# Every dense float32 product of a two-layer graph network written as two products of 64 columns of the tensor array

## The chip, the cores and the metric

The kernel runs on one core of a Trainium2 chip. The metric is the time on the device in microseconds (us), the median of repeated runs.

Names used below: PE is the tensor engine, PEld its weight loads, DVE the vector engine, ACT the scalar engine, POOL the GpSimd engine. A "slot" is the 429 ns that lie, in these traces, between the starts of two records of PE with 512 columns of a float32 operand; a float32 product leaves two records, one slot each.

## The reference

Two layers over a batch of 32 graphs of 512 nodes with 512 features, all float32. Layer 0 is masked attention with 8 heads of 64, layer 1 a graph attention whose logits are a sum of two vectors.

```python
# layer 0
h = relu(layernorm(x));  q, k, v = h @ Wq + bq, h @ Wk + bk, h @ Wv + bv      # 8 heads of 64
attn = softmax(q @ k.T / 8 + (1 - adj) * -1e9)
x = x + (attn @ v) @ Wo + bo
# layer 1
h = relu(layernorm(x));  g = h @ W;  s1, s2 = g @ a1, g @ a2
att = softmax(leaky_relu(s1[:, None] + s2[None, :], 0.2) * adj)
x = x + elu(att @ g + beta * g)
```

## The kernel before

PE's order is written by hand; the other engines follow a scheduler. While batch b is in its attention, PE also works on the projections of batch b+1 (pq, pk, pv), on the output projection of b-1 (pw) and on the second layer of b-2 (pg, py). These are the dense products: weights of 128 columns, four steps of accumulation. The functions that matter (lines left out are marked `# ...`):

```python
def proj_q(b, hT, f, qT):                       # proj_k, proj_v, out_proj, gather, final alike
    p = psum.tile([P, N], F32, name=f"pq_{b}_{f}", tag="mm")      # tag mm: two buffers
    for c in range(C):
        nc.tensor.matmul(p, wq[:, c, ts(f, P)], hT[c], start=c == 0, stop=c == C - 1)
    q = wtile([P, N], f"qT_{b}_{f}", "qT", 6)
    nc.vector.scalar_tensor_tensor(q, p, bq_c[:, f : f + 1], edge8, op0=ALU.add, op1=ALU.mult)
    # ...

def scores(b, j, k, st):                        # two heads: 64 rows of the array each
    # ...
    for s in range(2):
        rows = slice(s * HD, (s + 1) * HD)
        nc.tensor.matmul(p[:, s, :], st["kT"][j][rows, ts(k, P)], st["qT"][j][rows, :], start=True, stop=True)
    # ... mask on DVE, exp on ACT, sum on POOL

def attend(b, j, st):                           # two heads: 64 columns of the array each
    # ...
    for k in range(T):
        for s in range(2):
            nc.tensor.matmul(po[s * HD : (s + 1) * HD, :], v[k][:, (2 * j + s) * HD : (2 * j + s + 1) * HD],
                             e[k][:, s, :], start=k == 0, stop=k == T - 1)
    # ...
    for s in range(2):
        nc.tensor.matmul(pd[s * HD : (s + 1) * HD, :], ones[:, :HD], st["es"][j][:, s, :], start=True, stop=True)
    # ...

def residual(b, st):
    # ...
    for t in range(T):
        r = wtile([P, D], f"x1_{b}_{t}", "x1", 6)
        nc.sync.dma_start(r, x[b, ts(t, P), :])
        nc.gpsimd.tensor_tensor(r, r, c_row, op=ALU.add)          # c_row = bo + bv @ Wo
        st["x1"].append(r)

# out_proj, behind its product: DVE adds p to x1, statistics on DVE, power -0.5 on POOL, nb on DVE,
# hn on ACT, two reductions on DVE. logits: the reductions are spread by pbs (lg below), a product with ones.

        # dense(b): Y final, F projections pq/pk in turn, V pv, W out_proj, G gather, lg logits, D diagonal (pe), L loads
            order = (
                G + [Y[0], F[0], Y[1], F[1], W[0], Y[2], W[1], F[2], W[2], Y[3], W[3], F[3], F[4]]
                + L + [F[5]] + lg + [F[6], F[7]] + V[:2] + D + V[2:]
            )
```

## Time and profile before

| | before |
|---|---|
| time, median | 4092.1 us (4090.8 to 4092.1, 3 runs) |
| span of the profiled run | 4089.3 us, clock 0.993 |
| PE busy | 3950.5 us, 11616 records |
| changes of tiling in PE's records (without the one-column product of a check at the end) | 768 |
| PE's wait of pbs for DVE (qT) | 35.2 us, 28 times |

The lines stand in the prediction. Three things about reading them. An instruction's tiling is the pair in front of its shapes: `128*64` is 128 rows by 64 columns of the array. A busy time overlaps: records are longer (0.59 us) than their spacing, so PE's pace is read from starts. And a time "before" an instruction in brackets is idle time of the engine, with who ended it.

### The profile page before, as it was taken

Reading aid. Unit: us, or ns where it says so; the run is one execution under the profiler, and the core shown is the slowest. Engines: PE = TensorE matmul, PEld = TensorE weight load, DVE = VectorE, ACT = ScalarE, POOL = GpSimd, SP = SyncE. Lnnn points to the kernel's source line nnn. Section 1 sums busy time; section 2 is a strip of 40 time slices with the busy share of each in tenths; the row PEclk is TensorE's granted clock in tenths of the full one; section 3 lists DMA queues with packets and bytes.
Section 4 is the critical chain, followed back from the end, with each engine's and each line's share of the span. In section 5 each row is a group of like instructions: output and inputs, shape, how many; then the busy total and the mean of one; then the engine's idle time right before and its main releaser. Section 6 shows DMA issues by size and latency. Waiting matters only on the chain. (4 is left out here: it accounts for less than half of the span.)

```text
span 4089.3 us, 32221 instructions
## 1 busy us (share of the span) xinstructions
PE 3950.5 (97%) x11616; PEld 1590.1 (39%) x11616; DVE 2409.2 (59%) x3323; ACT 1254.4 (31%) x1799; POOL 1839.0 (45%) x1519
## 2 busy tenths in 40 slices
PE   6999999999999999999999999999999999999988
PEld 3333334333343333343333433333433334333333
DVE  4556655566655566555666555665556665556653
ACT  1333323333223333233332233332333322333331
POOL 2444544444444445444444444454444444444451
PEclk9999999999999999999999999999999999999989
DMA  3000000000000000000010000000000000000000
GB/s 116 11 16 26 21 31 28 25 21 31 21 31 26 26 21 21 31 27 26 21 31 21 31 26 22 26 21 31 28 25 21 31 21 31 26 26 11 21 21 27
DMA packets 59047, 109.90 MB, mean 27 GB/s; under 512 B 6464, under 2 KB 6464, under 8 KB 58880
## 3 DMA queue, kind: packets, MB, share of 16 engines
q1 hardware_dynamic: 55872, 101.74, 7.9%
q10 hardware_dynamic: 2640, 5.24, 0.4%
q8 instruction: 93, 1.52, 0.2%
q0 software_dynamic: 368, 0.79, 0.1%
q14 instruction: 74, 0.61, 0.0%
HBM read 74.19 MB, written 33.55 MB: 26 GB/s over the span
## 5 line engine op out<-in xcount | busy, mean ns | idle before, releaser
L264 POOL TENSOR_TENSOR es<-es,e 128x512 f32<-128x512 f32 x512 | 713.2, 1423 | 460.7 <-ACT e L257 460.7
L254 DVE TENSOR_TENSOR e<-ps,nmT 128x1024 f32<-128x1024 f32 x512 | 606.3, 1216 | 457.5 <-PE ps L250 453.2
L257 ACT ACTIVATE e<-e 128x1024 f32<-128x1024 f32 x512 | 540.5, 1056 | 920.3 <-DVE e L254 743.1
L285 DVE RECIPROCAL rd<-pd 128x512 f32<-128x512 f32 x128 | 429.4, 3355 | 443.3 <-PE pd L279 443.3
L250 PE MATMUL ps<-qT,kT 64*128 64x512 f32 x2048 | 519.9, 622 | 4.0 <-DVE e L254 3.2
L222 PE MATMUL pq<-hT,wq 128*128 128x512 f32 x1024 | 467.8, 600 | 14.6 <-ACT kT L234 13.9
L377 PE MATMUL py<-w,gT 128*128 128x512 f32 x1024 | 475.6, 608 | 0.3 <-DVE qT L224 0.3
L264 POOL TENSOR_TENSOR es<-e,e 128x512 f32<-128x512 f32 x256 | 343.8, 1363 | 282.5 <-ACT e L257 282.5
L272 PE MATMUL po<-e,v 128*64 128x512 f32 x2048 | 468.8, 600 | 0.0
L232 PE MATMUL pk<-hT,wk 128*128 128x512 f32 x1024 | 467.2, 599 | 0.8 <-DVE at L334 0.8
L303 PE MATMUL pw<-wo,oT 128*128 128x512 f32 x1024 | 462.5, 595 | 3.2 <-DVE x L307 3.2
L367 PE MATMUL pg<-at,hn 128*128 128x512 f32 x1024 | 458.5, 601 | 0.0
L240 PE MATMUL pv<-wv,hT 128*128 128x512 f32 x1024 | 455.3, 597 | 0.0
L288 POOL TENSOR_TENSOR oT<-oT,rd 128x512 f32<-128x512 f32 x128 | 171.3, 1338 | 625.2 <-DVE rd L285 544.8
L297 POOL TENSOR_TENSOR x<-x,c_row 128x512 f32<-128x512 f32 x128 | 165.0, 1290 | 378.1 <-DMA x<-in_x_dram 333.5
L323 DVE CUSTOM_DVE_ANT_0 scr<-hn,wa_r 128x512 f32<-128x512 f32 x256 | 267.8, 1083 | 68.9 <-ACT hn L317 68.9
L222 PEld LDWEIGHTS pq<-hT,wq 128*128 128x128 f32 x1024 | 189.9, 190 | 280.6 <-issue 213.4
L250 PEld LDWEIGHTS ps<-qT,kT 64*128 64x128 f32 x2048 | 174.9, 187 | 313.0 <-issue 218.3
L377 PEld LDWEIGHTS py<-w,gT 128*128 128x128 f32 x1024 | 186.3, 191 | 283.1 <-issue 235.4
L367 PEld LDWEIGHTS pg<-at,hn 128*128 128x128 f32 x1024 | 190.3, 191 | 264.7 <-issue 232.4
L232 PEld LDWEIGHTS pk<-hT,wk 128*128 128x128 f32 x1024 | 189.3, 190 | 265.7 <-issue 218.0
L303 PEld LDWEIGHTS pw<-wo,oT 128*128 128x128 f32 x1024 | 194.7, 191 | 251.4 <-issue 244.7
(95 smaller groups left out, 3213.7 us busy)
## 6 DMA issues: line engine op xcount, KB each, us to landing
x<-in_x_dram SPq DMA_DIRECT2D x256, 256.0 KB, 2.9
out_dram<-y SPq DMA_DIRECT2D x128, 256.0 KB, 2.9
wq<-in_L_gnn_Wq_dram ACTq DMA_DIRECT2D x1, 1024.0 KB, 7.5
wk<-in_L_gnn_Wk_dram ACTq DMA_DIRECT2D x1, 1024.0 KB, 14.4
adj<-in_adj_dram SPq DMA_DIRECT2D x4, 256.0 KB, 11.9
wv<-in_L_gnn_Wv_dram ACTq DMA_DIRECT2D x1, 1024.0 KB, 11.8
wo<-in_L_gnn_Wo_dram ACTq DMA_DIRECT2D x1, 1024.0 KB, 14.5
w<-in_L_gnn_W_dram ACTq DMA_DIRECT2D x1, 1024.0 KB, 12.9
```

Source lines behind the costliest of these rows:

```text
L222: nc.tensor.matmul(p, wq[:, c, ts(f, P)], hT[c], start=c == 0, stop=c == C - 1)
L232: nc.tensor.matmul(p, wk[:, c, ts(f, P)], hT[c], start=c == 0, stop=c == C - 1)
L240: nc.tensor.matmul(p, hT[c][:, ts(t, P)], wv[:, c, :], start=c == 0, stop=c == C - 1)
L250: nc.tensor.matmul(p[:, s, :], st["kT"][j][rows, ts(k, P)], st["qT"][j][rows, :], start=True, stop=True)
L254: nc.vector.tensor_tensor(e, p, nmT[:, k, :].unsqueeze(1).to_broadcast([P, 2, N]), op=ALU.add)
L257: nc.scalar.activation(e, e, AF.Exp)
L264: nc.gpsimd.tensor_tensor(es[:, s, :], one[:, s, :], e[:, s, :], op=ALU.add)
L272: nc.tensor.matmul(po[s * HD : (s + 1) * HD, :], v[k][:, (2 * j + s) * HD : (2 * j + s + 1) * HD], e[k][:, s, :], start=k == 0, stop=k == ...
L285: nc.vector.reciprocal(rd, pd)
L303: nc.tensor.matmul(p, st["oT"][c][:, ts(t, P)], wo[:, c, :], start=c == 0, stop=c == C - 1)
L367: nc.tensor.matmul(p, st["hn"][k][:, ts(c, P)], st["at"][k], start=k == 0, stop=k == T - 1)
L377: nc.tensor.matmul(p, st["gT"][c][:, ts(t, P)], w1[:, c, :], start=c == 0, stop=c == C - 1)
```

## The change

The intent is to have the dense products in the tiling of the value products (128*64), with both column halves of the array at work at once. The arithmetic is the same.

```diff
+def product(nc, out, lhsT, rhs, start=True, stop=True):
+    for s in range(0, out.shape[0], HD):
+        nc.tensor.matmul(out[s : s + HD], lhsT[:, s : s + HD], rhs, start=start, stop=stop)

     def proj_q(b, hT, f, qT):
         p = psum.tile([P, N], F32, name=f"pq_{b}_{f}", tag="mm")
         for c in range(C):
-            nc.tensor.matmul(p, wq[:, c, ts(f, P)], hT[c], start=c == 0, stop=c == C - 1)
+            product(nc, p, wq[:, c, ts(f, P)], hT[c], start=c == 0, stop=c == C - 1)
 ...  # the same in proj_k, proj_v, out_proj, gather, final, diagonal (pe), row_bcast (pbs) and row_constants
```

The transposes (pn), which stay 128*128, and the scores (ps), which stay 64*128, are untouched.

More of the change, by code (lines that the diff above doesn't have):

```diff
@@ L113, in row_bcast @@
         p = psum.tile([P, N], F32, name="pb" + name, tag="mm")
-        nc.tensor.matmul(p, ones, dg.rearrange("p t n -> p (t n)"), start=True, stop=True)
+        product(nc, p, ones, dg.rearrange("p t n -> p (t n)"), start=True, stop=True)
         return p
@@ L169, in row_constants @@
             nc.vector.tensor_copy(r, bv_c[:, c : c + 1].to_broadcast([P, P]))
-            nc.tensor.matmul(p, r, wo[:, c, :], start=c == 0, stop=c == C - 1)
+            product(nc, p, r, wo[:, c, :], start=c == 0, stop=c == C - 1)
         nc.vector.tensor_add(c_row, c_row, p)
@@ L231, in proj_k @@
         for c in range(C):
-            nc.tensor.matmul(p, wk[:, c, ts(f, P)], hT[c], start=c == 0, stop=c == C - 1)
+            product(nc, p, wk[:, c, ts(f, P)], hT[c], start=c == 0, stop=c == C - 1)
         k = wtile([P, N], f"kT_{b}_{f}", "kT", 6)
@@ L239, in proj_v @@
         for c in range(C):
-            nc.tensor.matmul(p, hT[c][:, ts(t, P)], wv[:, c, :], start=c == 0, stop=c == C - 1)
+            product(nc, p, hT[c][:, ts(t, P)], wv[:, c, :], start=c == 0, stop=c == C - 1)
         s = wtile([P, D], f"v_{b}_{t}", "v", 8)
@@ L302, in out_proj @@
         for c in range(C):
-            nc.tensor.matmul(
-                p, st["oT"][c][:, ts(t, P)], wo[:, c, :], start=c == 0, stop=c == C - 1
+            product(
+                nc, p, st["oT"][c][:, ts(t, P)], wo[:, c, :], start=c == 0, stop=c == C - 1
             )
@@ L349, in diagonal @@
         for t in range(T):
-            nc.tensor.matmul(pd[:, t, :], st["as"][:, ts(t, P)], ones[:, :HD], start=True, stop=True)
+            product(nc, pd[:, t, :], st["as"][:, ts(t, P)], ones[:, :HD], start=True, stop=True)
         bd = wtile([P, T], f"bd_{b}", "bd", 2)
@@ L366, in gather @@
         for k in range(T):
-            nc.tensor.matmul(
-                p, st["hn"][k][:, ts(c, P)], st["at"][k], start=k == 0, stop=k == T - 1
+            product(
+                nc, p, st["hn"][k][:, ts(c, P)], st["at"][k], start=k == 0, stop=k == T - 1
             )
@@ L376, in final @@
         for c in range(C):
-            nc.tensor.matmul(
-                p, st["gT"][c][:, ts(t, P)], w1[:, c, :], start=c == 0, stop=c == C - 1
+            product(
+                nc, p, st["gT"][c][:, ts(t, P)], w1[:, c, :], start=c == 0, stop=c == C - 1
             )
```

## The prediction

> **What bounds the kernel now.** I read the page first, its busy shares and the slices, then the costliest groups. Tensor engine (PE) is busy in nearly every slice; no other engine passes 59%.
>
> ```profile
> PE 3950.5 (97%) x11616; PEld 1590.1 (39%) x11616; DVE 2409.2 (59%) x3323; ACT 1254.4 (31%) x1799; POOL 1839.0 (45%) x1519
> PE   6999999999999999999999999999999999999988
> L222 PE MATMUL pq<-hT,wq 128*128 128x512 f32 x1024 | 467.8, 600 | 14.6 <-ACT kT L234 13.9
> L250 PE MATMUL ps<-qT,kT 64*128 64x512 f32 x2048 | 519.9, 622 | 4.0 <-DVE e L254 3.2
> L272 PE MATMUL po<-e,v 128*64 128x512 f32 x2048 | 468.8, 600 | 0.0
> ```
>
> Three tilings of the array are in use: 128*128 (six dense groups like pq, 1024 records each; a float32 product leaves two), 64*128 (scores ps) and 128*64 (value products po and the denominators pd). Note that 2048 of the half-width records cost what 1024 full ones do: 468.8 against 467.8 us. So they must run two at a time. The busy share hides the question that matters, which is the spacing of starts, so I went to the timeline of PE in one batch, and to that of the weight loads.
>
> ```profile
> 1961.78 3.65 PE L272 MATMUL po<-e,v 128*64 128x512 f32 x16
> 1965.26 1.03 PE L279 MATMUL pd<-es,ones 128*64 128x512 f32 x4
> 1966.22 3.70 PE L232 MATMUL pk<-hT,wk 128*128 128x512 f32 x8
> 1969.76 3.60 PE L222 MATMUL pq<-hT,wq 128*128 128x512 f32 x8
> 1973.28 1.99 PE L250 MATMUL ps<-qT,kT 64*128 64x512 f32 x8
> 1975.20 3.70 PE L232 MATMUL pk<-hT,wk 128*128 128x512 f32 x8
> 1980.09 1.13 PE L114 MATMUL pbs<-dgs,ones 128*128 128x512 f32 x2 [1.18 <-DVE qT L224]
> ...
> 2004.50 1.11 PE L350 MATMUL pe<-ones,as 128*128 128x64 f32 x8
> 2005.45 7.08 PE L240 MATMUL pv<-wv,hT 128*128 128x512 f32 x16
> 2012.37 0.60 PE L214 MATMUL pn<-ident,x 128*128 128x128 f32 x4
> 2013.22 1.15 PE L214 MATMUL pn<-ident,x 128*128 128x128 f32 x8 [0.25 <-ACT v L242]
> ```
>
> ```profile
> 2006.36 0.19 PEld L240 LDWEIGHTS pv<-wv,hT 128*128 128x128 f32 x1 [0.24 <-issue]
> 2006.79 0.19 PEld L240 LDWEIGHTS pv<-wv,hT 128*128 128x128 f32 x1 [0.24 <-issue]
> 2007.22 0.19 PEld L240 LDWEIGHTS pv<-wv,hT 128*128 128x128 f32 x1 [0.24 <-issue]
> ```
>
> ```profile
> 400.54 0.20 PEld L272 LDWEIGHTS po<-e,v 128*64 128x64 f32 x4 [0.76 <-issue]
> 401.02 0.14 PEld L272 LDWEIGHTS po<-e,v 128*64 128x64 f32 x2 [0.29 <-issue]
> 401.45 0.14 PEld L272 LDWEIGHTS po<-e,v 128*64 128x64 f32 x2 [0.28 <-issue]
> ```
>
> The reader is to subtract starts. Inside a dense group records start every 0.43 us (2006.36, 2006.79, 2007.22). Inside po *two* start every 0.43 us (401.02, 401.45). So 16 po records are 8 slots, not 16. But groups take longer than their slots: po and pd, 10 slots or 4.29 us, occupy 1961.78 to 1966.22 = 4.44; the pk after them, 8 slots or 3.43 us, takes to 1969.76 = 3.54. The surplus is the change of tiling, and it is what this edit can win.
>
> I took the start-to-start times of all records of the trace, sorted by tiling and by place after a change of tiling (medians). A slot without a change is 429 ns, in both tilings. Into po: the last dense slot grows to 522 (+93), and po's first slot to 480 (+51). Out of pd: its last slot grows to 529 (+100), the first dense slot to 533 (+104). Into ps from a dense group: +93, then +104. Out of ps: +96, then +104. There are 128 visits to po and pd and 256 to ps.
>
> [...] +93 to +100 ns at each change. [...] the second surplus, a load not hidden behind a running matmul, is 104 ns where 128 columns enter and 51 where 64 do. [...]
>
> **The change part by part.** Every full-width product becomes two over the two halves of the columns, issued one after the other with the same moving rows, just like the two heads in po. The program's Matmult rows on PE rise, the order of products does not; on the other engines only one DVE operation changes place. Nothing is removed from DVE, ACT, POOL or the queues.
>
> (a) *Within a dense group: nothing.* One slot of 429 ns per full product becomes one slot of two halves, as in po. Four records per slot in place of two; the loads are shorter (0.14 against 0.19 us) and stay hidden.
>
> (b) *Changes around po and pd vanish.* Dense and po are now both 128*64. 93 + 51 + 100 + 104 = 348 ns a visit, times 128 visits = 44.5 us.
>
> (c) *Out of ps into dense: a cheaper first load.* 51 in place of 104, in 227 of the 256 exits (29 go to pe): 227 x 53 ns = 12.0 us. Into ps [...] 100 against 93, from 195 dense groups: 1.4 us lost.
>
> (d) *pe, the small products with a moving operand of 64 columns.* Their 8 slots take 112 ns each, about the load of 128 columns. Two loads of 64 columns start together in po's entry (the row x4 above: four loads within 0.20 us), so a slot could drop to about 60 ns, if instructions are issued that fast: 4 in 60 ns. Gain 0 to 0.42 us a batch; I take 0.25, times 32 = 8 us.
>
> (e) *Added: a change of tiling in front of the transposes pn*, which stay 128*128. Some 0.15 us in 31 batches [...]. But after four transposes PE idles 0.25 us for ACT's last v, a time set by the end of pv; the delay fits in that. 0 us.
>
> (f) *Lost again in the wait of pbs.* The view of waits has for PE:
>
> ```profile
> PE pbs L114 <- DVE qT L224: 35.2, 28, 2.6
> PE pq L222 <- ACT kT L234: 13.9, 26, 0.5
> PE pn L214 <- ACT v L242: 7.5, 30, 0.3
> ```
>
> pbs needs a PSUM buffer that DVE empties (qT) after a chain of its own: from the end of the last pw at 1961.78 through statistics, POOL's power, hn and two reductions to 1979.3. DVE idles 3.3 us for POOL inside this chain, so it is latency and not PE's pace. What PE saves between that pw and pbs it then waits: one po visit (348) plus one exit of ps (53) less 7 = 394 ns, times 29 = 11.4 us.
>
> Sum: 44.5 + 12.0 - 1.4 + 8 - 11.4 = 51.7 us. I take off 5 us for waits that the trace does not show yet since they are hidden behind PE today: 47 us. 4092 - 47 = **4045 us**, 1.1% less.
>
> **The rivals.** *The two halves don't overlap.* If they ran one after the other, 6144 dense slots of 429 ns would double: +2600 us. Against it: po and pd, 10 slots in a row, run exactly so, paired. Untested is only that both halves stream the same moving rows, and long stretches. I give it 3%. *Issue becomes the bound.* PE would have to take four instructions in 429 ns, 107 ns each, for 20 us on end. Po with pd prove it for 40 instructions only[...]; transposes, at 110 ns for a load and a matmul, run twice that rate for 16. If a slot became 450 ns, 6144 x 21 = +129 us, 3% slower. I give it 4%. *PE's savings all turn into waits.* DVE at 59% and POOL at 45% aren't full, and only pbs, pq and pn wait in each batch; the gain would stay at 20 us: 4072. *The clock.* The wait of pbs grows from about 1.2 to 1.6 us. Were that enough to halve the clock in every batch, 3.4 us at half pace would cost 1.7 us, times 30 = 51 us, and the whole gain is gone: 4095. The longest such wait now, 2.6 us, with a mean clock of 0.993, speaks against it. *All of it counts*, pe's full 13 us included, with no new waits: 44.5 + 12 + 13 = 70: 4022. More than 2%, 82 us, would need something that I don't see in the trace.
>
> **Range and chances.** The ends follow from these: nothing lost at one end, most of it at the other: 4024 to 4072. Faster by over 2%: 6%; within 2%: 87%; slower by over 2%: 7% (the two rivals of issue and overlap).
>
> **What would show it.** In the profile after: the dense groups as 128*64 with twice the records and nearly the same busy time; starts of loads in pairs every 0.43 us in pv (a); pd followed by pk with no surplus: pk's 8 slots in 3.43 us in place of 3.54 (b); the first slot after ps at 0.48 (c); eight pe slots in well under 0.9 us (d); pn's idle for v gone (e); the wait of pbs grown by about 0.4 us a batch, some 11 us in all (f); a clock near 0.99. Wrong would be: a slot over 430 ns in long dense stretches, a clock below 0.97, or a new waiter among PE's waits with over 15 us.

## The result

The changed kernel takes 4040.4 us (4040.0 to 4041.7, 4 runs), the one before 4091.4 in the same rounds: 51.0 us less. The ratio is 0.9876 (95% interval 0.9859 to 0.9893). Ratios here are the mean time of one kernel's fast runs over the mean of the other's of the same rounds, so they are not quite the ratio of the medians that are quoted.

The page after, PE's busy row and the groups that answer to those of before (all dense groups now carry the helper's line, L38; the columns behind the bars are busy us and mean ns, then idle time before):

```profile
PE 3886.6 (96%) x18094; PEld 1303.7 (32%) x18094; DVE 2428.3 (60%) x3323; ACT 1258.4 (31%) x1799; POOL 1843.7 (46%) x1519
L257 PE MATMUL ps<-qT,kT 64*128 64x512 f32 x2048 | 522.4, 625 | 6.1 <-DVE e L261 4.1
L38 PE MATMUL pq<-hT,wq 128*64 128x512 f32 x2048 | 464.6, 596 | 13.9 <-ACT kT L241 12.9
L279 PE MATMUL po<-e,v 128*64 128x512 f32 x2048 | 462.6, 594 | 0.0
```

Twice the dense records, and nearly the same busy time: 2048 records of pq take 464.6 us where 1024 took 467.8. The timeline of PE after, in one batch (start, length, group, number of records):

```profile
1935.75 3.60 PE L279 MATMUL po<-e,v 128*64 128x512 f32 x16
1939.19 1.03 PE L286 MATMUL pd<-es,ones 128*64 128x512 f32 x4
1940.04 3.60 PE L38 MATMUL pk<-hT,wk 128*64 128x512 f32 x16
1943.48 1.89 PE L38 MATMUL pq<-hT,wq 128*64 128x512 f32 x8
...
1954.34 1.08 PE L38 MATMUL pbs<-dgs,ones 128*64 128x512 f32 x4 [1.76 <-DVE qT L231]
...
1978.36 0.69 PE L38 MATMUL pe<-ones,as 128*64 128x64 f32 x16
1978.88 7.04 PE L38 MATMUL pv<-wv,hT 128*64 128x512 f32 x32
1985.85 2.76 PE L221 MATMUL pn<-ident,x 128*128 128x128 f32 x16
```

The weight loads of pv after, in the timeline:

```profile
1975.06 0.14 PEld L38 LDWEIGHTS pv<-wv,hT 128*64 128x64 f32 x2 [0.29 <-issue]
1975.49 0.14 PEld L38 LDWEIGHTS pv<-wv,hT 128*64 128x64 f32 x2 [0.29 <-issue]
```

And PE's waits after, the two that recur in each batch (us in total, times, longest):

```profile
PE pbs L38 <- DVE qT L231: 51.5, 28, 3.2
PE pq L38 <- ACT kT L241: 12.9, 24, 0.5
```

Subtracting starts: po with pd, 10 slots, now occupies 1935.75 to 1940.04 = 4.29 us, where it was 4.44. The pk after it takes 3.44, where it was 3.54: no surplus is left on either side. Loads come in pairs every 0.43 us. The group pe takes 0.52 us to the next start, where it was 0.95. The transposes run as one piece of 16, without the idle 0.25 us. And the wait of pbs has grown from 35.2 to 51.5 us.

### The profile page after: what moved, and what is told of

It is laid out like the page before. It is cut to its first block, busy times and chain, and to the rows that moved or that the text cites. A ratio compares the mean times of both kernels' runs of the same rounds, so it can differ in the third digit from the quotient of the medians.

```text
span 4038.4 us, 45341 instructions
## 1 busy us (share of the span) xinstructions
PE 3886.6 (96%) x18094; PEld 1303.7 (32%) x18094; DVE 2428.3 (60%) x3323; ACT 1258.4 (31%) x1799; POOL 1843.7 (46%) x1519
## 5 line engine op out<-in xcount | busy, mean ns | idle before, releaser
L38 PE MATMUL pq<-hT,wq 128*64 128x512 f32 x2048 | 464.6, 596 | 13.9 <-ACT kT L241 12.9
L38 PE MATMUL py<-w,gT 128*64 128x512 f32 x2048 | 467.6, 599 | 0.5 <-DVE qT L231 0.5
L38 PE MATMUL pw<-wo,oT 128*64 128x512 f32 x2048 | 462.8, 594 | 3.3 <-DVE x L314 3.3
L38 PE MATMUL pk<-hT,wk 128*64 128x512 f32 x2048 | 463.0, 594 | 1.1 <-DVE at L341 1.1
L38 PE MATMUL pg<-at,hn 128*64 128x512 f32 x2048 | 453.7, 596 | 0.0
L38 PE MATMUL pv<-wv,hT 128*64 128x512 f32 x2048 | 450.8, 593 | 0.0
L393 POOL TENSOR_TENSOR y<-y,x 128x512 f32<-128x512 f32 x128 | 162.4, 1269 | 290.4 <-DVE y L392 290.4
L38 PEld LDWEIGHTS pq<-hT,wq 128*64 128x64 f32 x2048 | 141.3, 137 | 321.0 <-issue 259.6
L38 PEld LDWEIGHTS pw<-wo,oT 128*64 128x64 f32 x2048 | 147.0, 137 | 298.0 <-issue 291.6
L279 PEld LDWEIGHTS po<-e,v 128*64 128x64 f32 x2048 | 147.4, 138 | 292.8 <-issue 292.2
```

Of the source, the lines that this page charges most:

```text
L38: nc.tensor.matmul(out[s : s + HD], lhsT[:, s : s + HD], rhs, start=start, stop=stop)
L393: nc.gpsimd.tensor_tensor(y, y, st["x1"][t], op=ALU.add)
```

## The experiments

Twelve kernels were run, each correct on these inputs; the time of each is compared with the kernel before in the same rounds.

| run | tiling of dense | other edit | time, us | against before, us | ratio |
|---|---|---|---|---|---|
| the change | 64 | | 4040.4 | -51.0 | 0.9876 |
| e1_proj | pq, pk, pv 64; rest 128 | | 4100.1 | +10.7 | 1.0026 |
| e2_rest | pw, pg, py 64; rest 128 | | 4087.5 | -1.9 | 0.9992 |
| e3_pe_full | 64, pe 128 | | 4058.8 | -30.6 | 0.9925 |
| e4_apart | 64 | halves of pq, pk, pv apart | 4362.2 | +272.7 | 1.0666 |
| e5_order_full | 128 | new order | 4070.9 | -19.6 | 0.9952 |
| e6_order_split | 64 | new order | 4018.1 | -72.4 | 0.9821 |
| e7_quarters | 32, po and pd too | | 4038.2 | -52.3 | 0.9874 |
| e8_noadd_full | 128 | no addition of c_row | 4007.8 | -81.9 | 0.9800 |
| e9_noadd_split | 64 | no addition of c_row | 3956.2 | -133.5 | 0.9675 |
| e10_noadd_order | 64 | no addition, new order | 3938.2 | -151.5 | 0.9631 |
| e11_noadd_order | 128 | no addition, new order | 4024.0 | -65.0 | 0.9842 |
| e12_dve_add | 64 | addition on DVE, new order | 4011.2 | -77.8 | 0.9810 |

The theory was that all of the gain is made where the tiling changes, plus pe. The rival was that a split product is cheaper in itself: its weight loads are shorter, and PEld's busy time did fall from 1590 to 1304 us.

**e1_proj and e2_rest: half of the dense products each.** If the products themselves were cheaper, each half would bring half of the gain.

```diff
 # e1_proj: out_proj, gather, final, diagonal, the broadcasts and row_constants go back to
-            product(nc, p, ...)
+            nc.tensor.matmul(p, ...)
 # e2_rest: the same for proj_q, proj_k, proj_v, diagonal, the broadcasts and row_constants
```

> Only the three projections (pq, pk, pv) are split, half of the dense products; pw, pg, py and pe stay 128 columns wide. Theory (the gain is made where the tiling changes): the changes are moved, not removed; by the order of the groups in the trace of before there are now 880 changes for 768, and with +93 to +100 ns for each, +104 ns for each first load of 128 columns and +51 for each of 64 the kernel is some 16 us SLOWER, about 4108 (range 4095 to 4120). Rival (a split product is cheaper in itself, by its shorter weight load): half of the 51 us is gained, about 4066.

> The other half is split: pw, pg and py; the projections and pe stay wide. Theory (changes of tiling): 735 changes for 768, some 7 us faster, about 4085 (range 4075 to 4095); this and the run with only the projections split do not add up to the 51 us of the whole change. Rival (a split product is cheaper in itself): about 4066, and the two halves add up.

The first half costs 10.7 us, the second gains 1.9 with an interval of the ratio that includes 1 (0.9979 to 1.0006). Together that is 8.8 us *more*, where the whole change brings 51.0 less. The records have the expected numbers of changes of tiling: 880 and 735, for 768 before and 546 in the changed kernel. So the rival falls: the gain belongs to the changes of tiling, and half of the edit only moves them. Both times are some 5 us off the figures expected: e1_proj gained and e2_rest lost that much.

**e3_pe_full: what pe is worth.**

```diff
-            product(nc, pd[:, t, :], st["as"][:, ts(t, P)], ones[:, :HD], start=True, stop=True)
+            nc.tensor.matmul(pd[:, t, :], st["as"][:, ts(t, P)], ones[:, :HD], start=True, stop=True)
```

> The changed kernel with pe alone kept 128 columns wide. Theory: pe's slots go back from 58 to 112 ns (some 13 us) and a change of tiling is added behind pe (100 ns and a first load of 51, some 5 us): 18 us slower than the changed kernel, about 4058. Rival (pe lies beside waits and its cost is hidden): within 4 us of the changed kernel, about 4041.

It gains 30.6 us against before, so 20.4 of the 51.0 are gone; 18 were expected. The 16 records of pe start in pairs 58 ns apart when split; when whole, its 8 records start 112 ns apart. Behind this whole pe the first pv starts 205 ns after the last pe record, where it was 112 in the kernel before, and its first slot is 480 ns.

**e4_apart: does it matter that the halves are neighbours in the program?**

```diff
 # pq, pk, pv: in the kernel this is a helper, written out here for pq
-        for c in range(C):
-            product(nc, p, wq[:, c, ts(f, P)], hT[c], start=c == 0, stop=c == C - 1)
+        for s in range(0, 128, HD):                     # all of one half, then all of the other
+            for c in range(C):
+                nc.tensor.matmul(p[s : s + HD], wq[:, c, ts(f, P)][:, s : s + HD], hT[c], start=c == 0, stop=c == C - 1)
```

> The changed kernel, but in pq, pk and pv all eight records of the first 64 columns come before all eight of the second. Theory A (PE starts matmuls in the order of the program, so only neighbours in that order overlap): these groups take nearly twice as long, 15 slots in place of 8, 12 groups a batch, 7 x 0.43 us x 384 = +1150 us, about 5190. Theory B (PE takes a later matmul for a free tile ahead of an earlier one): no difference, about 4040.

It is neither: 323.7 us slower than the changed kernel, not 1150, and not equal. The weight loads at the start of two pv groups (PEld's timeline; the first line holds the first two loads of the first half):

```profile
2014.52 0.20 PEld L46 LDWEIGHTS pv<-wv,hT 128*64 128x64 f32 x2
2015.01 0.14 PEld L46 LDWEIGHTS pv<-wv,hT 128*64 128x64 f32 x1 [0.29 <-issue]
2015.44 0.14 PEld L46 LDWEIGHTS pv<-wv,hT 128*64 128x64 f32 x1 [0.29 <-issue]
2015.87 0.14 PEld L46 LDWEIGHTS pv<-wv,hT 128*64 128x64 f32 x1 [0.29 <-issue]
2016.30 0.19 PEld L46 LDWEIGHTS pv<-wv,hT 128*64 128x64 f32 x3 [0.29 <-issue]
```

and, in PE's timeline, a place where value products and denominators meet:

```profile
2002.44 0.59 PE L291 MATMUL pd<-es,ones 128*64 128x512 f32 x1
2002.81 0.59 PE L284 MATMUL po<-e,v 128*64 128x512 f32 x1
```

For four slots one half runs alone; at 2016.30 the other half joins (three loads in one line), though three of the first half's eight records have yet to start. So in this run PE does start a later matmul ahead of earlier ones, by some three or four records; the po record after a pd record, against the program's order, shows the same. Four slots run half empty at the start of a stretch and four at its end, so each stretch between two changes of tiling loses about four slots, 1.72 us. The changed kernel has 220 such stretches with a pq, pk or pv in them: an estimate of 378 us, less the wait of pbs for qT (51.5 us in the changed kernel), which is no longer among PE's waits in this run, makes 326. Measured: 323.7. (The wait of pq for kT falls as well, from 12.9 to 0.5 us; with it the estimate is 314, so that the closeness of 326 is in part luck.) Within the change the halves stand side by side, and neither matters.

**e7_quarters: is there room in the issue?** All pieces 32 columns wide, po and pd too, so that there is one tiling again.

```diff
-    for s in range(0, out.shape[0], HD):
-        nc.tensor.matmul(out[s : s + HD], lhsT[:, s : s + HD], rhs, start=start, stop=stop)
+    for s in range(0, out.shape[0], 32):
+        nc.tensor.matmul(out[s : s + 32], lhsT[:, s : s + 32], rhs, start=start, stop=stop)
 # and product() in attend for po and pd
```

> Every product, the value products and denominators too, in pieces of 32 columns, four at a time: all of it in one tiling again. Theory [...]: a further 5 us faster than the changed kernel, about 4035. Rival (issue becomes the bound: eight loads and matmuls in 429 ns, 54 ns each): slots over 429 ns and a slower kernel, over 4080; at 60 ns an instruction a slot is 480 ns, some +370 us.

The weight loads of pg in this run's timeline:

```profile
2000.48 0.13 PEld L38 LDWEIGHTS pg<-at,hn 128*32 128x32 f32 x4 [0.30 <-issue]
2000.91 0.13 PEld L38 LDWEIGHTS pg<-at,hn 128*32 128x32 f32 x4 [0.30 <-issue]
```

Four loads and four matmuls in each 0.43 us, with no slot inside a group longer: issue was not a bound at 128*64, nor at twice its rate. The slot behind a change from ps is 453 ns in place of 480, so its surplus over 429 is 24 ns in place of 51. But the slot ahead of a change to ps is 543 ns in place of 529 (a surplus of 114 in place of 100), which takes about half of that back. The theory's 5 us were my estimate. Whether the kernel is faster for it stays open: 1.3 us more gain, from another chip's rounds, is within the intervals.

**e5_order_full and e6_order_split: can the wait of pbs be gone by order?** Step (f) of the prediction said that the wait takes back part of the gain. In the new order the groups ahead of pbs are emptied by ACT and not by DVE.

```diff
-                ... W[3], F[3], F[4]] + L + [F[5]] + lg + [F[6], F[7]] + V[:2] + D + V[2:]
+                ... W[3], F[3], V[0]] + L + [F[5]] + lg + [F[4], F[7], F[6]] + V[1:2] + D + V[2:]
```

> The kernel before, with only the order of dense groups changed: the groups ahead of pbs are now pk, pv, pk (emptied by ACT) and pq comes after it, so pbs's buffer no longer waits for DVE's chain. Theory: the wait of pbs, 35 us, is gone and nothing takes its place: about 4055 (range 4040 to 4065). Rival (the wait moves to the next group that needs DVE): no change, 4085 to 4095.

> The changed kernel with the same new order. Theory (16 us of what PE saved were lost in the wait of pbs): its wait of 51 us is gone, about 3988, and the gain of the split in this order, against the wide kernel in the same order, is 51 + 16 = about 67 us. Rival (the wait of pbs grew for a reason of its own, such as a slower DVE): the gain of the split stays at about 51 us.

Both expectations of the theory failed; e5_order_full lies between its theory and its rival. The two kernels gain 19.6 and, over the change, 21.4 us, and the gain of the split stays at 72.4 - 19.6 = 52.8. Among PE's waits, pbs for qT is gone, and in its place stands, in e5_order_full:

```profile
PE ps L250 <- DVE e L254: 26.4, 30, 3.2
```

and in e6_order_split:

```profile
PE ps L257 <- DVE e L261: 41.8, 30, 2.9
```

The next scores need a buffer that DVE empties, and DVE is still late. The wait is a meeting of PE with DVE's chain; it moved to the next meeting, with its difference between the kernels (15 us) kept. What makes DVE late? In the kernel before, POOL's timeline just ahead of the power that the chain needs:

```profile
1962.63 1.28 POOL L386 TENSOR_TENSOR y<-y,x 128x512 f32<-128x512 f32 x1
1967.19 1.26 POOL L297 TENSOR_TENSOR x<-x,c_row 128x512 f32<-128x512 f32 x1 [3.28 <-DMA x<-in_x_dram]
1968.41 0.55 POOL L191 TENSOR_TENSOR rs<-rs,mhalf 128x1 f32<-128x1 f32 x1
```

and DVE's:

```profile
1969.00 0.16 DVE L315 SCALAR_TENSOR_TENSOR nb<-mv,rs 128x1 f32<-128x1 f32 x1 [3.30 <-POOL rs L191]
```

POOL finishes with a residual tile (L386), the next load goes into that buffer, and POOL, in order, stands 3.28 us for it, since the scheduler put the addition of c_row (for a later batch, not urgent) ahead of the power, whose input DVE (L190) had written by 1964.96. DVE stands 3.30 us for the power.

**e8 to e11: take that addition away.** The four kernels are right only where bo and bv are zero, as in these inputs.

```diff
             nc.sync.dma_start(r, x[b, ts(t, P), :])
-            nc.gpsimd.tensor_tensor(r, r, c_row, op=ALU.add)
```

> The kernel before without POOL's addition of c_row to the residual tiles (right for these inputs, whose output and value biases are zero, but wrong for others). In both kernels POOL, in order, idles 3.3 us for the next residual load just ahead of the power that DVE's chain needs. Theory (that chain's latency sets the start of pbs): the chain is 3.3 us shorter than a wait of 1.2, so the wait of pbs is gone: 4092 - 35 = about 4057 (range 4045 to 4065). Rival (DVE's own work sets it): within 8 us of 4092.

> The changed kernel without that addition (the same reserve). Theory: its wait of pbs, 51 us, is gone too: about 3989 (range 3980 to 4000), so the split gains 51 + 16 = about 67 us against the wide kernel without the addition: the 16 us that went into the wait come out. Rival (the wait grew for a reason of the split itself): the gain stays at about 51 us.

> The changed kernel without the addition and with the new order of dense groups as well. Theory: the wait is already gone, so the order gives nothing more: within 8 us of the run without the addition alone. Rival (a second wait on DVE behind the first): 20 us faster, as the order alone was.

> The wide kernel (as before) without the addition and with the new order: the mate of the changed kernel with both, 3938. Theory (where no DVE-fed wait is left in either kernel, the split shows its whole PE gain): nothing more than the 4008 of the wide kernel without the addition, range 4000 to 4012, so the split gains 68 to 70 us, near the sum of its PE terms (44.5 + 12.0 - 1.4 + 13 = 68). Rival (the order is worth its 18 to 20 us here too and the split never gains more than 51): about 3990.

In e8_noadd_full every wait for DVE and ACT in mid-batch except the transposes' is gone; what recurs is only this:

```profile
PE pn L214 <- ACT v L242: 7.5, 30, 0.3
PE pn L214 <- ACT hT L216: 6.0, 30, 0.2
```

So the chain was the cause, but I had its price too low: 81.9 us, not 35, for with it go the wait of pq for kT (13.9 us) and the stretched slots around both. Summed from start to start, pk is 38.1 us shorter than before, ps 30.0, pc (once, near the start of the kernel) 5.3, pw 5.1 and pbs 4.7. The run takes away the stall and the addition's own 1.3 us together and does not part them. From the last pw to the dgs that feeds pbs, the median is 11.8 us, where it was 15.2.

In e9_noadd_split a new wait appears:

```profile
PE pk L38 <- DVE at L340: 14.7, 28, 1.1
```

so the split again shows 133.5 - 81.9 = 51.6 us and the expected 67 don't come out. With the new order as well, e10_noadd_order has 1.3 us of that wait in 2 places and is 18.0 us faster, against the theory I had written for it. And its mate e11_noadd_order, the wide kernel in the new order, now has such a wait:

```profile
PE pk L232 <- DVE at L333: 11.3, 29, 0.8
```

and is 4024 us in place of the 4008 expected. In the same order, then, the split gains 51.6 us where the split kernel meets the wait, and 151.5 - 65.0 = 86.5 where the wide one does. The pair in which *neither* has a wait for DVE in each batch is e8_noadd_full and e10_noadd_order, from the same chip's rounds, though in different orders of groups: 151.5 - 81.9 = **69.6 us**. The sum of the PE terms without (f), with pe at its measured size, is 44.5 + 12.0 - 1.4 + 13.9 = 69.0.

What this shows: the split frees some 70 us of PE, and meetings with DVE hand back 17 to 19 of them. What stays open: no pair in one and the same order is free of waits on both sides, so the 70 rests on a pair that differs in order too.

**e12_dve_add: a version that is right for all inputs.** The addition moves behind the output projection, on DVE, with the new order and the split.

```diff
         nc.vector.scalar_tensor_tensor(x1, p, 1.0 / VS, x1, op0=ALU.mult, op1=ALU.add)
+        nc.vector.tensor_tensor(x1, x1, c_row, op=ALU.add)
```

> Right for all inputs: the changed kernel, the new order, and the addition of c_row moved from POOL ahead of the load's use to DVE behind the output projection, 128 operations of about 0.65 us. Theory (DVE's chain now has some 4.7 us to spare before pbs): nearly all of 3938 is kept, 3938 to 3950. Rival (83 us more on DVE bring the waits back): 3960 or more.

It is the fastest kernel that is right for all inputs, 4011.2 us, 1.9% under the kernel before, and it missed the theory: most of what the addition's removal brought is gone again. DVE's groups and PE's waits in this run:

```profile
L314 DVE TENSOR_TENSOR x<-x,c_row 128x512 f32<-128x512 f32 x128 | 109.0, 852 | 4.3
```

```profile
PE ps L257 <- DVE e L261: 37.5, 30, 1.3
PE pq L38 <- ACT kT L241: 15.6, 29, 0.6
```

The addition takes 852 ns and not the 650 that I had set as an estimate (dgs, the same operation at the same shape, has a median of 652 in the kernel before), and DVE is late again by the same measure as with POOL's stall: from the last pw to dgs the median is 15.3 us, as in e6_order_split. The spare time that I counted on was spent.

## Why the prediction was right

The predicted time was 4045, the measured one 4040.4, and the steps can be checked one by one.

(a) Right in what it says of time: a slot of two halves takes 429 to 430 ns (medians) in every dense group after, over stretches of 32 records; e7_quarters shows room to spare. Its words slip: a float32 product takes two slots and not one, so there are two records a slot in place of one.

(b) Right, by number. The changes around po and pd are gone: the slot into po is 429 ns where 522 was, the last one of pd 429 where 529 was. e1_proj and e2_rest show that it is the change, since splitting half of the groups brings nothing (+10.7 and -1.9 us).

(c) Right. The first dense slot after ps is 480 ns in place of 533, 53 less, to 1 ns in 225 of the 227 places. That the surplus is a load which nothing hides fits PEld's starts: around ps, po and pd the second load behind a change starts 108 ns after the first where 128 columns are loaded, and the second pair 55 after the first pair where 64 are (medians), while inside a group a load starts with the matmul ahead of its own (2 ns after it, median of pk). Into ps the slot ahead is 529 ns (522 before), and the first of ps 534 in both kernels.

(d) The mechanism was right, the size too small: I took 0.25 us a batch out of a range of 0 to 0.42, and the pe groups went from 33.5 to 19.6 us by starts, 13.9 us in all, or 0.43 a batch; the load that nothing hides ahead of pe is shorter too (its first slot 107 ns, where it was 160), which the range left out. The instructions do issue fast enough, 58 ns for a pair with its two loads.

(e) Right. The surplus in front of pn is there (530 ns for the last slot of pv, then 165 for the first transpose in place of 110; why these 55 are not 104, with 128 columns loaded, is not shown), and both waits of pn, 7.5 and 6.0 us, are gone; the pn groups take 88.4 us by starts where they took 90.7, about what the longer pv slots in front of them cost.

(f) The mechanism was right, the size too small: 11.4 us were set, and the two rows of pbs's wait for DVE grew from 46.9 to 64.3, by 17.4. PE's part came out as worked out, the stretch from the last pw to the last record ahead of pbs falls from 17.06 to 16.66 us (medians), 395 ns for 394. But pbs itself came 0.07 us later after that pw (18.90 in place of 18.83), while DVE takes up the pw result 0.15 us later (why is not shown), and in a few batches it is 1.4 us later. In each of the 28 batches with the wait, in both kernels, pbs starts 11.62 to 11.63 us after the end of POOL's addition of c_row, and POOL's stall on the load ahead of it, 3.30 us in both medians, is over 3.7 us in five batches after (up to 4.8) and in two before, 2.8 us more in all. Why those loads landed later is not shown. What I called the chain's latency was POOL's stall on a load, as e8_noadd_full shows, and I had not named that.

With the measured sizes the sum is 44.5 + 12.0 - 1.4 + 13.9 - 17.4 = 51.6, and 51.0 was measured. The predicted sum, 51.7, is as close by luck: (d) was 5.9 us too small and (f) 6.0, and the two errors cancel. The deduction of 5 us for unseen waits was not needed; it is what parts 4045 from 4040.4.

The rivals: the halves do overlap (two in each slot of 429 to 430 ns), and issue is no bound (four loads and four matmuls in 0.43 us in e7_quarters). The rival of the clock came true in small, though the mean is still 0.992. Between 110 and 3800 us the clock records hold two windows of 3.41 us at half clock in the kernel before and four in the changed one. Each begins 0.3 to 1.7 us after the start of a pbs that had waited 1.7 to 3.2 us, and from that pbs to the next pq it takes 4.36 to 4.72 us in place of 3.93: 1.1 us in all before, 2.8 after. So a window costs 0.4 to 0.8 us and not 1.7, and far from every batch has one. The eight kernels without a wait of pbs for qT in each batch (e4_apart, e5_order_full, e6_order_split, e8 to e12) have no such window in this stretch. That the wait causes them is argued from this, not shown.

## What to carry to other kernels

Where tilings of the array alternate, count the changes and price each from the trace's starts, here 93 to 100 ns on the slot ahead of a change and, on the first slot behind it, 104 where the products load 128 columns and 51 where they load 64; bringing *all* groups between them to one tiling removes them, and doing part of it only moves them. Halves that shall overlap stand side by side in the program (apart, in e4_apart, they cost 323.7 us). Before summing what a busy engine saves, look for the next place where it meets a late one: there the saving turns into a wait, and taking the wait out by order alone moves it to the next meeting (26.4 and 41.8 us in e5_order_full and e6_order_split) unless the cause of the lateness goes.
